# One allocator for the eight PSUM banks of a two-layer scan and attention kernel

## The chip, the core and the metric

The kernel is one program on one core of a Trainium2 chip, launched once, with all arithmetic on the chip. The metric is device time in microseconds, from the first to the last instruction; lower is better. The time before is the median of three runs, 1815.26 us (1812.67 to 1815.69).

## What is computed

Two layers, each an attention-like part and a feed-forward part, each part followed by a residual sum and a layer norm, on 2048 tokens (2 batches of 1024) of width 512, all in float32. Cut to what matters:

```
x = layernorm(x + lightning_attention(x))     # 16 heads of 32, decay per head, chunks of 128
x = layernorm(x + ffn0(x))                    # silu(x W1) * (x W3), Hadamard transform, W2; 512 -> 2048 -> 512
x = layernorm(x + selective_scan(x))          # h = exp(delta A) h + delta u B;  y = sum over 32 states of h C;  + u D
x = layernorm(x + ffn1(x))                    # silu(x Wg) * (x Wu), Wd; 512 -> 2048 -> 512

def step(h, inp):                             # the scan, per token; state is 512 channels x 32
    delta_t, B_t, C_t, u_t = inp
    dA = exp(delta_t[:, :, None] * A[None])
    h = dA * h + (delta_t * u_t)[:, :, None] * B_t[:, None, :]
    return h, einsum('bdn,bn->bd', h, C_t)
```

## The kernel before

**Tiling.** The 2048 tokens are cut into five groups of 256, 512, 512, 512 and 256 tokens (`GROUPS`). Each group runs through phases: V (values), A (attention), F (first feed-forward), the scan, and f (second feed-forward; two of the second ones are split into halves a1 and b1). Phases of different groups overlap: while VectorE (DVE), ScalarE (ACT) and GpSimd (POOL) run the scan of one group, TensorE (PE) runs the attention and feed-forward matmuls of others.

**The scan** of a group of 512 tokens has 64 units, each for one state and two blocks of 128 channels; a group of 256 tokens has 32 units, each for one state and four blocks. Per unit, POOL writes `dbu` = du * B (L1392), ACT writes `da` = exp(delta * a) block by block into PSUM (L1412: two instructions of 512 columns, or four of 256), DVE scans each block in place in PSUM (L1440), ACT keeps the last column for the next group of the same batch (L1465, which only reads `da`), and DVE multiplies `da` by C into `dbu` (L1453, which only reads `da` as well). POOL and a DMA with addition sum the results (L1483, L1489, L299).

**PSUM** has eight banks of 128 x 512 float32. The pool `ps` (L229) gives two kinds of tiles: `mm`, one bank, four buffers (L244), for every matmul output, and `da`, two banks, two buffers (L245), for the scan alone. Each use of a buffer is a tile of its own: `ps.tile(...)` is called anew for each one.

**Who reads an `mm` bank.** A matmul group is four matmuls of 512 columns (or eight of 256) into one bank. In a feed-forward phase (L1052) banks hold the gate and the up product in turn; ACT takes the silu of the one (L501), DVE multiplies by the other (L1083). The down product (L1106) is added to the residual by DVE (L1125). In attention the groups are shorter: transposes, state updates, scores, gate, outputs and norms (L729, L795, L845, L766, L891, L900, L936), read by DVE (L736, L813 and L815, L863, L919, L952) and ACT (L778, L945). Transposes (L527) are copied by ACT (L534).

**The order of work** is made when the program is built. `Order` holds one generator (thread) per phase and helper; each yields operations with an engine, an estimated duration, what is read and written, and which buffers are allocated. `run` (L166) repeatedly puts the operation that can start earliest by these estimates; `begin` (L106) says when an operation can start, among other things by when a buffer of its tag becomes free, and `put` (L129) takes the buffer, emits the instructions and moves the estimated clocks. So the emission order, and with it the order on each engine, follows estimated start times. The framework below (`manual_schedule`) keeps that order on each engine and adds the semaphore waits itself, from what the emitted instructions read and write of each tile.

`decays` (L1403) is the thread that emits the exponentials and `steps` (L1428) the one that emits the scans and products; each starts when the scan of the group before has finished with it.

Of the kernel before, what the change touches and what calls it, by code (L numbers as in the profile page):

```python
# [9 lines left out]
F32 = mybir.dt.float32  # L10
# [3 lines left out]
PSUM = bass.MemoryType.PSUM  # L14
DRAM = bass.MemoryType.DRAM

P = 128
# [3 lines left out]
G = 512  # L21
# [54 lines left out]
        self.r, self.w, self.a, self.free, self.spare = r, w, a, free, spare  # L76


class Order:


# [16 lines left out]
        self.now = 0.0  # L98

    def tag(self, name, n, make):  # L100
        self.tags[name] = (n, make, [])

    def spawn(self, gen, prio=0):
        self.new.append([gen, prio, None])

    def begin(self, op, spare=True):  # L106

        t = self.free[op.eng]
        for b in op.r:
            if b.written is None:  # L110
                return None
            t = max(t, b.written + self.HOP)
        for b in op.w:
            t = max(t, b.last + self.HOP)
        for name in {name for name, _ in op.a}:
            n, _, bufs = self.tags[name]
            k = sum(name == v for v, _ in op.a) + (op.spare if spare else 0) - (n - len(bufs))
            if k > 0:
                free = sorted(b.last for b in bufs if b.refs <= 0)
                if len(free) < k:  # L120
                    return None
                t = max(t, free[k - 1] + self.HOP)
        return t

    def switches(self, op):
# [2 lines left out]

    def put(self, op, t):  # L129
        for name, b in op.a:  # L130
            n, make, bufs = self.tags[name]
            if len(bufs) == n:
                bufs.remove(min((v for v in bufs if v.refs <= 0), key=lambda v: v.last))
            b.t = make()
            bufs.append(b)
        op.fn()
        us = op.us
        if self.switches(op):
            us += 1.3
            self.table = op.table[0]  # L140
        end = self.free[op.eng] = t + us
        if op.dma:
            q = max(self.queue[op.eng], end + 0.9) + op.dma / (
                self.QUEUE if t > self.ALONE else self.FIRST
            )
            self.queue[op.eng] = q
            end = q + 0.9
        for b in op.r:
            b.last = max(b.last, end)
        for b in op.w:  # L150
            b.last = b.written = max(b.last, end)
        for _, b in op.a:
            b.last = b.written = end
        for b in op.free:
            b.refs -= 1
        self.now = max(self.now, t)
# [56 lines left out]
def two_layers(  # L213
# [8 lines left out]
    order = Order()  # L222
# [3 lines left out]
    cp = ctx.enter_context(tc.tile_pool(name="cp", bufs=1))  # L226
    xp = ctx.enter_context(tc.tile_pool(name="xp", bufs=3 * CG))
    sm = ctx.enter_context(tc.tile_pool(name="sm", bufs=12))
    ps = ctx.enter_context(tc.tile_pool(name="ps", bufs=4, space=PSUM))  # L229
    dr = ctx.enter_context(tc.tile_pool(name="dr", bufs=1, space=DRAM))  # L230
    ring = ctx.enter_context(tc.tile_pool(name="ring", bufs=RING))

# [1 line left out]
    at = ExitStack()  # L234
# [6 lines left out]
    def tagged(name, n, pool, shape):  # L241
        order.tag(name, n, lambda: pool().tile(shape, F32, tag=name, name=name, bufs=n))

    tagged("mm", 4, lambda: ps, [P, 512])  # L244
    tagged("da", 2, lambda: ps, [P, 2, G])  # L245
    tagged("xT", 2, lambda: gp, [P, EB * G])
    tagged("xf", 1, lambda: gp, [P, EB * G // 2])
    tagged("h", 10, lambda: gp, [P, G])
# [14 lines left out]
    def chunks(gi):  # L263
        return GROUPS[gi][2]
# [8 lines left out]
    def begins(gi):  # L273
        return GROUPS[gi][1] == 0

    def ends(gi):
        return GROUPS[gi][1] + GROUPS[gi][2] == N // P
# [8 lines left out]
    def dve(cols, fn, **kw):  # L286
        return Op("DVE", 0.145 + cols * 1.05e-3, fn, **kw)

    def act(cols, fn, **kw):
        return Op("ACT", 0.18 + cols * 0.81e-3, fn, **kw)  # L290

    def pool(cols, fn, **kw):
        return Op("POOL", 0.15 + cols * 2.25e-3, fn, **kw)
# [74 lines left out]
    def take(ph, n):  # L368

        mine = of_phase[ph]  # L370
        bufs = [b for _, b, _ in mine[:n]]
        del mine[:n]
        return bufs
# [56 lines left out]
    def load_consts():  # L430
# [32 lines left out]
        def decays():  # L463
# [6 lines left out]

        raw = Buf()
        yield Op("ACT", 2.0, decays, r=[consts_b, early_b], w=[decays_b], table=EXP)
        yield dma(
            65536, lambda: a_s, lambda: alog.rearrange("(k p) n -> p k n", p=P), w=[raw]
# [28 lines left out]
    class Columns:  # L503


        def __init__(self, gi, tag="xT", cs=None):
            self.gi, self.tag = gi, tag
            self.cs = list(range(chunks(gi))) if cs is None else cs
            self.T = len(self.cs) * P
            self.whole = Buf()  # L510
            self.parts = [Buf() for _ in self.cs]
# [518 lines left out]
    def ffn(ph, xT, store, prio=0):  # L1030
# [5 lines left out]
        for fh, nt in enumerate(parts):  # L1036
# [36 lines left out]
            def hidden(f):  # L1073

                t, pg, pu = hT[f], pss[f, 0], pss[f, 1]
                yield act(
                    512, lambda: silu(t.t, pg.t), r=[pg], a=[(tag, t)], free=[pg], table=SILU
                )
                t.written = None
                if ending and f == nt - 1:  # L1080
                    reached(ph)
                yield dve(
                    512, lambda: nc.vector.tensor_mul(t.t, t.t, pu.t), r=[pu], w=[t], free=[pu]  # L1083
                )
# [128 lines left out]
    class Scan:  # L1213
# [3 lines left out]
        def __init__(self, gi):  # L1217
# [6 lines left out]
            ]  # L1224
            U = len(self.units)
            self.M = U // 2
            KP = 2 // self.R
            self.du, self.delta = [Buf() for _ in range(KP)], [Buf() for _ in range(KP)]
            self.bs, self.cs = [Buf() for _ in range(self.M)], [Buf() for _ in range(self.M)]
            self.db = [Buf() for _ in range(U)]  # L1230
            self.da = [Buf(1 if ends(gi) else 2) for _ in range(U)]
            self.ys = [Buf(), Buf()]
# [152 lines left out]
        def products(self):  # L1385
            if self.gi:
                yield lambda: scans[self.gi - 1].multiplied
            U = len(self.units)
            for i, (n, k0) in enumerate(self.units):
# [5 lines left out]
                    r=[du, bs], a=[("dbu", self.db[i])],  # L1395
                    free=([bs] if i % 2 else []) + ([du] if i + len(self.du) >= U else []),
                    prio=1,
# [5 lines left out]
        def decays(self):  # L1403
            if self.gi:
                yield lambda: scans[self.gi - 1].decayed
            U = len(self.units)
            for i, (n, k0) in enumerate(self.units):
                da, delta = self.da[i], self.delta[k0 // self.W]
                for j in range(self.W):
                    def exp():  # L1410
                        d = da.t.rearrange("p a (r t) -> p (a r) t", r=self.R)
                        nc.scalar.activation(  # L1412
                            d[:, j, :], self.wide(delta)[:, j, :], AF.Exp,
                            scale=a_s[:, k0 + j, n : n + 1],
                        )

                    yield act(
                        self.T, exp, r=[delta, scan_b] + ([da] if j else []),
                        a=[] if j else [("da", da)],
                        free=[delta] if i + len(self.delta) >= U and j == self.W - 1 else [],  # L1420
                        table=EXP,
                    )
                    self.dec[i, j].written = order.free["ACT"]
            self.decayed = True
# [3 lines left out]
        def steps(self):  # L1428
            gi, units, T = self.gi, self.units, self.T
            if gi:  # L1430
                yield lambda: scans[gi - 1].stepped
            for i, (n, k0) in enumerate(units):
                da, db, cs = self.da[i], self.db[i], self.cs[i // 2]
                d = lambda: da.t.rearrange("p a (r t) -> p (a r) t", r=self.R)
                for j in range(self.W):
                    def scan():
                        init = 0.0
                        if not begins(gi):
                            init = hlast[GROUPS[gi][0]][:, n, k0 + j : k0 + j + 1]
                        nc.vector.tensor_tensor_scan(  # L1440
                            d()[:, j, :], d()[:, j, :], self.wide(db)[:, j, :],
                            init, ALU.mult, ALU.add,
                        )

                    yield Op(
                        "DVE", 0.145 + T * 2.15e-3, scan, r=[self.dec[i, j], db, da],
                        w=[self.scanned[i]], prio=1,
                    )
                if not ends(gi):
                    spawn(self.keep_last(i))  # L1450

                yield dve(
                    1024, lambda: nc.vector.tensor_mul(  # L1453
                        self.wide(db), d(), self.row(self.cs, i)
                    ),
                    r=[da, cs], w=[db, self.out[i]], free=[da] + ([cs] if i % 2 else []), prio=1,
                )
            self.stepped = True

        stepped = False  # L1460

# [198 lines left out]
```

## Time and profile before

| | |
|---|---|
| median of the runs | 1815.26 us (1812.67 to 1815.69) |
| span of the profiled execution (the page gives no other time of it) | 1815.4 us, 0.14 us above the median |
| instructions in it | 21241 |
| granted TensorE clock, mean | 0.988 |
| busy PE, DVE, ACT, POOL | 1771.1, 1282.1, 1163.7, 1096.7 us |
| PE busy from 0 to 300 us | 290.3 us |
| PE busy from 300 to 1670 us, in which the scans lie | 1341.8 us |
| PE busy from 1670 us to the end | 139.0 us |

How to read it: the profile is of one execution. A line number is that of the kernel before. Lists of groups give engine, operation, tiles, shapes and count, then busy time and mean duration of one, then the idle time of that engine just before them and what ended it. One matmul of the kernel is two rows of the profile, so 24 matmuls appear as x48. The timeline gives the start, the duration, and in brackets the idle time before with its releaser. PEclk is the granted clock of TensorE as a share of full speed.

### The profile page before, as it was taken

The numbers are of one execution on the slowest core, as the hardware profiler recorded it, in microseconds if no ns is written. First come the engines' busy times: TensorE is split into PE (matmuls) and PEld (weight loads), VectorE is DVE, ScalarE is ACT, GpSimd is POOL, SyncE is SP. The second block draws the span as 40 slices with busy tenths as digits, with TensorE's granted clock in tenths as the row PEclk, the third lists the DMA queues.
The fourth block names the chain that finished last, engine by engine and source line by source line (L and its number), as shares of the span: only waits on it lengthen the run. The fifth ranks groups of instructions, "written<-read, shape, count | busy, mean of one in ns | idle before, by whom it ended". The sixth has DMA issues, their size and how long they took to land.

```text
span 1815.4 us, 21241 instructions
## 1 busy us (share of the span) xinstructions
PE 1771.1 (98%) x7064; PEld 1004.1 (55%) x7064; DVE 1282.1 (71%) x1537; ACT 1163.7 (64%) x1832; POOL 1096.7 (60%) x595
## 2 busy tenths in 40 slices
PE   8999999998999999999999999999999999999998
PEld 5456764443467644444666444676865444544574
DVE  3643115987599899944899999539999899998211
ACT  3734046688876676869767767686766868775311
POOL 2000015887577899935779989337998998776000
PEclk9999999999999999999999999999999999999999
DMA  9542435766648778745587787467989874766251
GB/s 283 156 139 82 151 118 168 197 164 175 210 128 253 206 207 233 200 119 185 154 221 221 199 231 212 143 213 236 275 241 262 204 213 159 199 172 168 81 174 58
DMA packets 225421, 336.32 MB, mean 185 GB/s; under 512 B 19569, under 2 KB 128897, under 8 KB 225313
## 3 DMA queue, kind: packets, MB, share of 16 engines
q1 hardware_dynamic: 206192, 270.86, 47.2%
q0 software_dynamic: 16816, 59.92, 17.6%
q10 hardware_dynamic: 2304, 4.20, 0.6%
q8 instruction: 56, 0.92, 0.2%
q14 instruction: 53, 0.43, 0.1%
HBM read 253.12 MB, written 22.54 MB: 152 GB/s over the span
## 4 chain that ended last, share of the span: by engine, by line
PE 67%; DVE 10%; ACT 8%; DMA 7%; POOL 4%; issue 3%; SPq 1%; DVEq 0%; POOLq 0%
PE mm L1052 36%; PE mm L1106 17%; DVE da L1440 6%; PE mm L658 4%; DMA y<-dbu 4%; POOL dbu L1392 3%; PE mm L1003 2%; ACT da L1412 2%; DVE dbu L1453 2%; PE mm L607 2%; ACT L501 1%; ACT L1412 1%; PE mm L845 1%; PE mm L1254 1%; PE mm L936 1%
## 5 line engine op out<-in xcount | busy, mean ns | idle before, releaser
L1392 POOL TENSOR_TENSOR dbu<-du,B 128x1024 f32<-128x1024 f32 x256 | 649.6, 2561 | 124.2 <-DMA y<-dbu 92.8
L1052 PE MATMUL mm<-xT,w 128*128 128x512 f32 (+1 forms) x1912 | 668.1, 510 | 2.9 <-ACT h L501 2.5
L1052 PEld LDWEIGHTS mm<-xT,w 128*128 128x128 f32 x1912 | 363.6, 191 | 303.9 <-issue 266.3
L1412 ACT ACTIVATE da<-delta,a_s 128x512 f32<-128x512 f32 (+1 forms) x640 | 384.4, 605 | 148.2 <-DVE dbu L1453 117.7
L1440 DVE TENSOR_TENSOR_SCAN da<-da,hlast,dbu 128x512 f32<-128x512 f32 (+1 forms) x384 | 425.8, 1109 | 36.9 <-ACT da L1412 27.7
L1489 POOL TENSOR_TENSOR y<-y,dbu 128x1024 f32<-128x1024 f32 x123 | 323.6, 2631 | 55.2 <-DVE dbu L1453 49.7
L1106 PE MATMUL mm<-w,h 128*128 128x512 f32 x768 | 339.4, 595 | 3.5 <-DMA w<-w2h 1.8
L1453 DVE TENSOR_TENSOR dbu<-da,C 128x1024 f32<-128x1024 f32 x256 | 312.9, 1222 | 13.9 <-ACT hlast L1465 7.0
L1440 DVE TENSOR_TENSOR_SCAN da<-da,dbu 128x256 f32<-128x256 f32 (+1 forms) x256 | 246.0, 961 | 26.7 <-ACT da L1412 18.8
L1106 PEld LDWEIGHTS mm<-w,h 128*128 128x128 f32 x768 | 145.2, 191 | 177.2 <-issue 164.4
L1052 PE MATMUL mm<-xf,w 128*128 128x256 f32 x1024 | 231.2, 385 | 0.2 <-DVE sc L863 0.2
L1052 PEld LDWEIGHTS mm<-xf,w 128*128 128x128 f32 x1024 | 196.7, 194 | 33.2 <-issue 4.6
L501 ACT ACT_TABLE_LOAD x143 | 183.5, 1283 | 5.1 <-PE mm L1052 2.3
L501 ACT ACTIVATE h<-mm 128x512 f32<-128x512 f32 x144 | 85.7, 597 | 114.3 <-PE mm L1052 66.3
L1083 DVE TENSOR_TENSOR h<-h,mm 128x512 f32<-128x512 f32 x96 | 65.2, 679 | 111.2 <-PE mm L1052 105.7
L1412 ACT ACT_TABLE_LOAD x109 | 139.8, 1283 | 1.9
L658 PE MATMUL mm<-xT,w 128*128 128x512 f32 (+1 forms) x320 | 116.6, 513 | 3.8 <-DVE sc L863 1.3
L299 POOL DMA_DIRECT2D y<-dbu x113 | 109.1, 966 | 12.4 <-DMA y<-dbu 5.1
L1465 ACT COPY hlast<-da 128x2 f32<-128x2 f32 (+1 forms) x160 | 25.4, 159 | 141.0 <-DVE dbu L1453 120.5
L1106 PE MATMUL mm<-w,hf 128*128 128x512 f32 x256 | 112.8, 592 | 0.0
L748 POOL TENSOR_TENSOR qd<-h,q_dec 128x512 f32<-128x512 f32 x14 | 17.8, 1271 | 151.0 <-ACT h L501 83.0
L1125 DVE TENSOR_TENSOR xn<-mm,xn 128x512 f32<-128x512 f32 x60 | 40.9, 681 | 92.9 <-PE mm L1106 92.5
(100 smaller groups left out, 1358.2 us busy)
## 6 DMA issues: line engine op xcount, KB each, us to landing
y<-dbu POOLq DMA_DIRECT2D x113, 512.0 KB, 6.0
w<-in_wgut_dram SPq DMA_DIRECT2D x192, 256.0 KB, 4.6
B<-rows SPq DMA_DIRECT2D x128, 256.0 KB, 4.6
C<-rows SPq DMA_DIRECT2D x128, 256.0 KB, 4.2
w<-in_wdnt_dram SPq DMA_DIRECT2D x96, 256.0 KB, 4.8
w<-in_w1t_dram SPq DMA_DIRECT2D x80, 256.0 KB, 4.7
w<-in_w3t_dram SPq DMA_DIRECT2D x80, 256.0 KB, 5.0
w<-w2h SPq DMA_DIRECT2D x80, 256.0 KB, 4.2
```

What stands on the lines that cost most here:

```text
L299: return Op(eng, us, lambda: of.dma_start(dst(), src(), **more), dma=nbytes, **kw)
L501: nc.scalar.activation(dst, src, AF.Silu)
L658: nc.tensor.matmul(bank.t[:, s * T : (s + 1) * T], w_qk[j][k].t[:, eb * P : (eb + 1) * P], xT.t[:, k, :], start=k == 0, stop=k == EB - 1,)
L1052: nc.tensor.matmul(bank.t[:, s * T + c0 * P : s * T + c1 * P], blocks[fb // 2][j][k // 2].t[:, k % 2 * 2 * P + k0 : k % 2 * 2 * P + k0 + P ...
L1083: 512, lambda: nc.vector.tensor_mul(t.t, t.t, pu.t), r=[pu], w=[t], free=[pu]
L1106: nc.tensor.matmul(accs[c].t, hT[f // S].t[:, s * T + c * P : s * T + (c + 1) * P], w_d[f].t, start=f == 0, stop=f == nt * S - 1,)
L1125: nc.vector.tensor_add(xb.t, bank.t, xb.t)
L1392: 1024, lambda: nc.gpsimd.tensor_mul(self.wide(self.db[i]), self.wide(du), self.row(self.bs, i)),
L1412: nc.scalar.activation(d[:, j, :], self.wide(delta)[:, j, :], AF.Exp, scale=a_s[:, k0 + j, n : n + 1],)
L1440: nc.vector.tensor_tensor_scan(d()[:, j, :], d()[:, j, :], self.wide(db)[:, j, :], init, ALU.mult, ALU.add,)
L1453: 1024, lambda: nc.vector.tensor_mul(self.wide(db), d(), self.row(self.cs, i)),
L1489: 1024, lambda: nc.gpsimd.tensor_add(y.t, y.t, db[i].t), r=o, w=[y],
```

## The change

Banks are no longer taken as tiles. The pool gives two tiles of four banks each, `mm` and `da`, allocated once, and every use takes a slice of one of them. A small allocator, `Banks`, remembers for each of the eight banks who holds it. Users of one bank may take any of the eight while no scan is open, and only the first four while one is; the scan takes bank pairs 4 and 6. A scan is open from when its `delta` is loaded (a new wait of the thread `decays`) until `steps` has emitted its last product. Where several banks are free, the one free longest is taken. The other tags keep their counts, in a class `Tiles` that does what `begin` and `put` did before.

```diff
+class Tiles:
+    def __init__(self, n, make):
+        self.n, self.make, self.bufs = n, make, []
+    def when(self, k):
+        k -= self.n - len(self.bufs)
+        if k <= 0:
+            return -1.0
+        free = sorted(b.last for b in self.bufs if b.refs <= 0)
+        return free[k - 1] if len(free) >= k else None
+    def take(self, b):
+        if len(self.bufs) == self.n:
+            self.bufs.remove(min((v for v in self.bufs if v.refs <= 0), key=lambda v: v.last))
+        b.t = self.make()
+        self.bufs.append(b)
+
+class Banks:
+    def __init__(self, views, usable):
+        self.views, self.usable = views, usable
+        self.holders = [None] * 8
+    def free_at(self, i):
+        b = self.holders[i]
+        return -1.0 if b is None else b.last if b.refs <= 0 else None
+    def of(self, width):
+        return BankTag(self, width)
+
+class BankTag:
+    def __init__(self, banks, width):
+        self.banks, self.width = banks, width
+    def places(self):
+        f, out = self.banks.free_at, []
+        for i in self.banks.usable(self.width):
+            at = [f(j) for j in range(i, i + self.width)]
+            if None not in at:
+                out.append((max(at), i))
+        return sorted(out)
+    def when(self, k):
+        free = self.places()
+        return free[k - 1][0] if len(free) >= k else None
+    def take(self, b):
+        at, i = self.places()[0]
+        b.t = self.banks.views(i, self.width)
+        for j in range(i, i + self.width):
+            self.banks.holders[j] = b
...
-        self.tags[name] = (n, make, [])
+        self.tags[name] = Tiles(n, make)
...
-            n, _, bufs = self.tags[name]
-            k = sum(name == v for v, _ in op.a) + (op.spare if spare else 0) - (n - len(bufs))
-            if k > 0:
-                free = sorted(b.last for b in bufs if b.refs <= 0)
-                if len(free) < k:
-                    return None
-                t = max(t, free[k - 1] + self.HOP)
+            k = sum(name == v for v, _ in op.a) + (op.spare if spare else 0)
+            free = self.tags[name].when(k)
+            if free is None:
+                return None
+            t = max(t, free + self.HOP)
...
-    ps = ctx.enter_context(tc.tile_pool(name="ps", bufs=4, space=PSUM))
+    ps = ctx.enter_context(tc.tile_pool(name="ps", bufs=1, space=PSUM))
...
-    tagged("mm", 4, lambda: ps, [P, 512])
-    tagged("da", 2, lambda: ps, [P, 2, G])
+    halves = [ps.tile([P, 4, G], F32, name=name) for name in ("mm", "da")]
+    opened = set()
+
+    def usable(width):
+        if width == 2:
+            return (4, 6)
+        return range(4 if opened else 8)
+
+    def views(i, width):
+        half = halves[i // 4]
+        return half[:, i % 4, :] if width == 1 else half[:, i % 4 : i % 4 + width, :]
+
+    banks = Banks(views, usable)
+    order.tags["mm"], order.tags["da"] = banks.of(1), banks.of(2)
...
+            yield lambda: self.delta[0].written is not None
+            opened.add(self.gi)
...
             self.stepped = True
+            opened.discard(self.gi)
```

## The prediction, as put on record before the changed kernel ran

> **What bounds the kernel now.** I read the page's busy times and slices first, then the chain of work, then the waits, then timelines.
>
> ```profile
> span 1815.4 us, 21241 instructions
> PE 1771.1 (98%) x7064; PEld 1004.1 (55%) x7064; DVE 1282.1 (71%) x1537; ACT 1163.7 (64%) x1832; POOL 1096.7 (60%) x595
> PE   8999999998999999999999999999999999999998
> PE 67%; DVE 10%; ACT 8%; DMA 7%; POOL 4%; issue 3%; SPq 1%; DVEq 0%; POOLq 0%
> ```
>
> TensorE (PE) is busy in all but 44 us: it is the bound, and it is nearly never late for a bank. So more banks can gain little. The PE gaps that end with a reader of a PSUM bank are the only ones that banks could shorten, and they are few: 2.5 us at L1052, 1.4 at L1106, 2.0 at L527 and a dozen under 1.3. Before the first scan PE idles 9.7 us, of which 8.4 us wait for first DMAs (4.45, 1.57, 2.39).
>
> What hides all other work is that PE runs the next group while DVE or ACT reads the bank of the last one. That holds because each use of a bank is now a tile of its own. What happens inside one tile, the scan's two-bank `da` tile shows:
>
> ```profile
> ACT hlast L1465 <- DVE dbu L1453: 120.5, 86, 3.0
> DVE dbu L1453 <- ACT hlast L1465: 7.0, 7, 1.2
> ```
>
> These are waits (total us, times, longest); next, the timeline:
>
> ```profile
> 1412.95 1.21 DVE L1453 TENSOR_TENSOR dbu<-da,C 128x1024 f32<-128x1024 f32 x1
> 1412.95 1.42 ACT L1412 ACTIVATE da<-delta,a_s 128x512 f32<-128x512 f32 x2
> 1414.47 2.62 DVE L1440 TENSOR_TENSOR_SCAN da<-da,hlast,dbu 128x512 f32<-128x512 f32 x2 [0.31 <-ACT da L1412]
> ```
>
> L1465 and L1453 only read `da`, and yet wait for each other. The first scan step at 1414.47 needs only the first exponential's bank, written by about 1413.66; DVE was free at 1414.16, and still it waited until the second exponential, in the tile's other bank, ended (1412.95 + 1.42 = 1414.37). So waits go by tile: accesses of one tile from two engines are ordered as emitted, whatever the bank, reads against reads included.
>
> **The change, part by part.** The counts of instructions stay: 3726 matmuls, 1539 on DVE, 1850 on ACT (321 table loads in both), 600 on POOL, 1009 on SP. SP and POOL issue the same DMAs in nearly the old order; at no cost, since no weight load moves ahead of a free buffer. The freedom to take eight banks while no scan is open touches only stretches that are not short of banks: worth 0 to 3 us (the sum of the few reader-ended gaps outside open scans), taken as 0.
>
> The costly part is that all uses are now slices of two tiles. I read the changed kernel's instruction order with its waits. In the four-bank tile `mm`, each of the 920 places where the emission order passes from one engine to another is ordered by a wait, and in 899 of them the two accesses are in different banks. Before, 634 of 666 were in the same bank. In the `da` tile it is 1243 places, 1038 across banks (before 500 and 275). PE resumes after another engine 436 times on `mm` and 81 on `da`: 517 handovers, 96 before the first scan, 396 while scans run, 25 after.
>
> What one handover costs: a reader of bank k is emitted after group k+1 of PE has been, because its estimated start is a hop later. So it waits for the end of group k+1, and group k+2, in another bank, waits for it. PE stands still for each reader. Behind a waiting reader on DVE stands the next scan step (L1440), for which ACT's next exponential waits, and for that the scan after it; on ACT the exponentials stand behind the silu. The durations come from these rows, of 512 columns:
>
> ```profile
> L1440 DVE TENSOR_TENSOR_SCAN da<-da,hlast,dbu 128x512 f32<-128x512 f32 x256 | 329.2, 1286 | 28.4 <-ACT da L1412 21.8 <-ACT hlast L1465 1.9 <-POOL dbu L1392 1.6
> L1453 DVE TENSOR_TENSOR dbu<-da,C 128x1024 f32<-128x1024 f32 x256 | 312.9, 1222 | 13.9 <-ACT hlast L1465 7.0
> L1412 ACT ACTIVATE da<-delta,a_s 128x512 f32<-128x512 f32 x384 | 263.3, 690 | 99.8 <-DVE dbu L1453 85.3 <-DVE da L1440 4.1 <-DMA delta<-dd 3.3
> ...
> L501 ACT ACT_TABLE_LOAD x143 | 183.5, 1283 | 5.1 <-PE mm L1052 2.3 <-ACT xn L565 0.4
> L501 ACT ACTIVATE h<-mm 128x512 f32<-128x512 f32 x144 | 85.7, 597 | 114.3 <-PE mm L1052 66.3 <-PE mm L658 28.7 <-PE mm L607 18.1
> L1083 DVE TENSOR_TENSOR h<-h,mm 128x512 f32<-128x512 f32 x96 | 65.2, 679 | 111.2 <-PE mm L1052 105.7 <-ACT h L501 4.6 <-issue 0.3
> ```
>
> A PE group is 3.46 us (the timeline has 12 in 41.60 us). A hop between DVE and ACT is 0.10 us (1414.37 to 1414.47 above); to or from PE 0.05:
>
> ```profile
> 838.66 0.60 ACT L501 ACTIVATE h<-mm 128x512 f32<-128x512 f32 x1
> 839.31 1.98 PE L658 MATMUL mm<-xT,w 128*128 128x512 f32 x4 [0.60 <-ACT h L501]
> ```
>
> With these I walked by hand through two stretches of the changed order, 17 handovers. The start of the first, a feed-forward beside a 512-token scan (us from the start of group A; the product before it ends at 1.00):
>
> ```
> PE   group A, bank 0           0.00- 3.46
> ACT  L1465 after L1453         1.10- 1.26
> DVE  L1440 after L1465         1.36- 2.64
> ACT  L1412 after L1440         2.74- 3.43
> DVE  L1083, bank 3, after A    3.51- 4.19
> PE   group B after L1083       4.24- 7.70   gap 0.78
> DVE  L1440                     4.19- 5.47
> ACT  L1412 after L1440         5.57- 6.26
> DVE  L1453 after L1412         6.36- 7.58
> ACT  L1465 after L1453         7.68- 7.84
> ACT  table load, L501, bank 0  7.84- 9.72
> PE   group C after L501        9.77-        gap 2.07
> ```
>
> Its gaps are 0.78, 2.07, 1.39, 1.55, 1.75, 2.08, 0.78, 1.18, and in a second stretch beside a scan without L1465 1.22, 0.78, 0.70, 0.78, 2.40, 0.78, 0.70, 1.12, 1.39: mean 21.45 / 17 = 1.26 us. A group thus takes 4.91 and 4.56 us instead of 3.46.
>
> The sum:
> - 396 handovers while scans run, at 1.26 us: 499 us.
> - 96 before the first scan and 25 after, at the smallest, a reader of 0.60 to 0.69 and two hops, 0.8 us: 97 us.
> - About 50 handovers hold two readers in a row (two score products L863, a silu and a copy); one more of 0.65 each: 33 us.
> - The clock. Where PE stood 2.51 us, it lost it:
>
> ```profile
> 1424.22 12.26 PE L1052 MATMUL mm<-xT,w 128*128 128x512 f32 x24 [2.51 <-ACT h L501]
> ```
> ```profile
> 1426.00:1428.00 2.00, 2.00 (x3) 0.76 (x3) 1.39 (x2) 1.95 (x4) 2.00 (x3) 0.50 0.95 230
> ```
>
>   In the second line, a window of 2 us, the granted clock is 0.50 (third number from the end), and the 12 matmuls took 12.26 instead of 10.4 us: 1.8 lost. A gap of 2.03 us at 1120 did the same, one of 1.77 at 673 did not. 3 of my 17 gaps exceed 2.0: 396 x 3/17 = 70 times 1.8 = 126 us.
>
> 499 + 97 + 33 + 126 = 755; less some 10 us of today's reader-ended gaps, 745. 1815.4 + 745 = **2560 us**. The profiled span is 0.1 us from the median, so no correction is made.
>
> A second way to it: the `da` tile's accesses in turn make a unit of 512 tokens 2 x 1.286 + 2 x 0.690 + 1.222 + 0.11 (L1465, where there is one) + 4.5 changes of engine x 0.10 = 5.7 us; in the walks, with readers between, it was 6.5 and 5.9. 192 such units at 6.2 are 1190 us, 64 of 256 tokens at an estimated 7.5 are 480: 1670 us, where the scans now lie in 1370 us together with pauses that add up to some 170. With the pauses and the stretches outside, stretched as above, that is about 2420, without clock losses. The two agree within 10%.
>
> Bounds: if each of the 517 handovers costs only 0.8 us, 1815 + 414 = 2230. If each costs the largest gap walked, 2.40, 1815 + 1241 = 3056. I take the walked mean, because it is from the order that will run.
>
> **Two rules of the Trainium skill.** The trace row of 1414.47 shows a wait across banks. "PSUM — Partial Sum Buffer", section "PSUM bank collisions raise a hardware error", says that two engines on different banks run clean, and that guarding by bank is enough. By that alone the chip needs none of the 899 waits, and the sum would be that of rival A. The instruction order has them nevertheless. "TensorE: Matmul & The Clock Gate", section "What's actually happening", lets the clock fall after an idle window of about 3.4 us; by that the clock term would be 0 and the sum 2434, while the rows lose it at 2.03 and 2.51 us.
>
> **Rivals.**
> - A, not slower. The waits are there, but their producers are done when PE comes, as four banks deep would give. PE then keeps its 98% and gains 0 to 3 us at its reader-ended gaps: 1813. For it: today's PE waits little for readers. Against it: the reader in question is the latest emitted, and itself waits for the group that has just ended. It decides from a gap under about 0.05 us; the least in my walk is 0.70. 3%.
> - B, mild. Each handover costs only reader and hops, because DVE and ACT, less loaded in a longer kernel, are always there, and the clock holds: 2230 (2150 to 2320). For it: DVE is 71% and ACT 64% busy. Against it: only 7 of 17 walked gaps were that small, as ACT's table loads stand before the silu. 11%.
> - C, two locked chains. Attention's short groups, with readers on both engines, table loads and half clock, bring the mean to the walk's largest gap: 2850 to 3056, taken as 2950. For it: the granted clock in attention is 0.50 to 0.66 already, at gaps of 0.6 to 1.2 us (1188 to 1192, 475 to 480). Against it: most handovers are of feed-forwards. 13%.
>
> The forecast, 2320 to 2850, has 73%. The range for 8 in 10 is widened a little into B: **2300 to 2850**, which leaves out C and most of B. Faster or slower means by over 0.2%, about what a measurement here can tell from no change: faster 1%, same 2% (rival A), slower 97%.
>
> **What would show it.** PE busy falls to 65 to 78% of the span while its matmul count stays; idle before L1052 and L1106, now 2.9 and 3.5 us, becomes hundreds, released by L501, L1083, L1125. DVE before L1440 waits for L1412 hundreds of us (now 46.5), ACT before L1412 for L1440. The readers' rows keep their durations. The clock shows 0.5 in parts. If PE stays above 90%, the reading of the waits is wrong; if PE's gaps are near 0.8 us, the scan's coupling is; if the clock's mean stays at 0.98, that term falls.

## The result, and the profile after

The changed kernel takes 2716.85 us (median of five runs, 2714.74 to 2720.15), the kernel before 1815.26 us on the same chip. The ratio is 1.498, with an interval of 1.496 to 1.500: 902 us slower. The forecast was 2560 us, in a range of 2300 to 2850.

The page of the changed kernel: span, busy times, the row of PE's slices, the granted clock of PE by slices, and the chain.

```profile
span 2715.1 us, 21523 instructions
PE 2044.9 (75%) x7064; PEld 1069.8 (39%) x7064; DVE 1310.3 (48%) x1537; ACT 1176.8 (43%) x1832; POOL 1101.7 (41%) x595
...
PE   8878977667667777676677787787777677677798
...
PEclk9999989887689999987699899898998899899999
...
PE 12%; DVE 10%; ACT 7%; issue 1%; DMA 0%; DVEq 0%; ACTq 0%; SPq 0%
```

The counts of matmuls and of the other engines' instructions stand where they stood, and PE, which was busy in all but 44 us, now idles in 670. DVE, ACT and POOL do the same work in the same busy time (DVE 28 us more), so nothing has become the new bound by load: no engine is above 75%. Such a page is that of engines that wait for one another. The chain could be followed back through only a third of the span, so it is not used here. PE's busy time itself grew by 274 us with the same 7064 rows, and the clock row has 6, 7 and 8 where it had 9: the second, smaller part of the loss. The mean granted clock is 0.903 (before 0.988).

The waits of the changed kernel (total us, times, longest):

```profile
ACT da L1479 <- DVE da L1507: 487.8, 241, 14.0
DVE da L1507 <- ACT da L1479: 400.4, 273, 11.4
...
ACT hlast L1533 <- DVE dbu L1520: 161.4, 94, 6.4
...
PE mm L1117 <- ACT h L566: 123.0, 65, 5.0
...
PE mm L1117 <- DVE h L1148: 72.9, 70, 2.5
...
PE mm L1171 <- DVE xn L1190: 54.5, 23, 6.4
```

Lines have moved by 65 to 68: L1117 and L1171 are the products L1052 and L1106, L566 the silu, L1148 and L1190 DVE's readers, L1479, L1507, L1520 and L1533 the exponential, the scan step, the product by C and the kept column. The exponential waits for the scan and the scan for the exponential, 241 and 273 times; that is the one `da` tile of four banks. PE waits for ACT's and DVE's readers of banks that its next group doesn't use; that is the one `mm` tile. The groups of instructions say the same from the side of the idle time (busy us, mean ns, idle us before it):

```profile
L1117 PE MATMUL mm<-xT,w 128*128 128x512 f32 x1120 | 558.2, 645 | 187.0 <-ACT h L566 107.7 <-DVE h L1148 64.0 <-DVE xn L1190 8.8
L1171 PE MATMUL mm<-w,h 128*128 128x512 f32 x672 | 341.0, 660 | 75.2 <-DVE xn L1190 46.3 <-ACT xT L599 12.0 <-ACT h L566 11.7
L1507 DVE TENSOR_TENSOR_SCAN da<-da,hlast,dbu 128x512 f32<-128x512 f32 x256 | 330.3, 1290 | 197.0 <-ACT da L1479 175.8 <-ACT hlast L1533 12.8 <-DVE dbu L1520 0.9
L1479 ACT ACTIVATE da<-delta,a_s 128x512 f32<-128x512 f32 x384 | 265.5, 691 | 391.7 <-DVE da L1507 342.0 <-DVE dbu L1520 42.5 <-ACT hlast L1533 0.6
L1148 DVE TENSOR_TENSOR h<-h,mm 128x512 f32<-128x512 f32 x90 | 61.5, 683 | 162.7 <-PE mm L1117 139.3 <-ACT h L566 8.9 <-PE mm L1336 6.8
```

The two matmul rows as they were before the change:

```profile
L1052 PE MATMUL mm<-xT,w 128*128 128x512 f32 x1160 | 502.6, 594 | 2.5 <-ACT h L501 2.5
L1106 PE MATMUL mm<-w,h 128*128 128x512 f32 x768 | 339.4, 595 | 3.5 <-DMA w<-w2h 1.8 <-DVE h L1083 1.4 <-ACT h L501 0.4
```

The means of DVE's and ACT's rows are nearly those of before (1290 after, 1286 before; 691 and 690; 683 and 679 ns): they wait and are not slowed. The matmul rows rose from 594 and 595 to 645 and 660 ns.

### The profile page after: what moved, and what is told of

Read it like the earlier page. It is cut to its first block, busy times and chain, and to the rows that moved or that the text cites. A ratio compares the mean times of both kernels' runs of the same rounds, so it can differ in the third digit from the quotient of the medians.

```text
span 2715.1 us, 21523 instructions
## 1 busy us (share of the span) xinstructions
PE 2044.9 (75%) x7064; PEld 1069.8 (39%) x7064; DVE 1310.3 (48%) x1537; ACT 1176.8 (43%) x1832; POOL 1101.7 (41%) x595
## 5 line engine op out<-in xcount | busy, mean ns | idle before, releaser
L1117 PE MATMUL mm<-xT,w 128*128 128x512 f32 (+1 forms) x1728 | 709.4, 560 | 236.6 <-ACT h L566 123.0
L1457 POOL TENSOR_TENSOR dbu<-du,B 128x1024 f32<-128x1024 f32 x256 | 628.1, 2467 | 39.3 <-DMA du<-dd 35.6
L1479 ACT ACTIVATE da<-delta,a_s 128x512 f32<-128x512 f32 (+1 forms) x640 | 387.9, 606 | 553.8 <-DVE da L1507 487.8
L1117 PEld LDWEIGHTS mm<-xT,w 128*128 128x128 f32 x1728 | 336.2, 202 | 607.9 <-issue 230.8
L1507 DVE TENSOR_TENSOR_SCAN da<-da,hlast,dbu 128x512 f32<-128x512 f32 (+1 forms) x384 | 427.2, 1113 | 271.7 <-ACT da L1479 246.7
L1557 POOL TENSOR_TENSOR y<-y,dbu 128x1024 f32<-128x1024 f32 x123 | 288.3, 2344 | 472.9 <-DVE dbu L1520 445.2
L1171 PE MATMUL mm<-w,h 128*128 128x512 f32 x672 | 341.0, 660 | 75.2 <-DVE xn L1190 46.3
L1520 DVE TENSOR_TENSOR dbu<-da,C 128x1024 f32<-128x1024 f32 x256 | 313.0, 1223 | 97.8 <-ACT da L1479 89.3
L1507 DVE TENSOR_TENSOR_SCAN da<-da,dbu 128x256 f32<-128x256 f32 (+1 forms) x256 | 246.8, 964 | 176.9 <-ACT da L1479 153.7
L1117 PE MATMUL mm<-xf,w 128*128 128x256 f32 x864 | 234.2, 432 | 55.0 <-DVE hf L1148 16.8
L1171 PEld LDWEIGHTS mm<-w,h 128*128 128x128 f32 x672 | 138.3, 212 | 265.1 <-issue 157.8
L1117 PEld LDWEIGHTS mm<-xf,w 128*128 128x128 f32 x864 | 184.6, 219 | 106.0 <-DVE hf L1148 23.3
L364 POOL DMA_DIRECT2D y<-dbu x113 | 98.6, 872 | 289.1 <-DVE dbu L1520 276.8
L1148 DVE TENSOR_TENSOR h<-h,mm 128x512 f32<-128x512 f32 x90 | 61.5, 683 | 162.7 <-PE mm L1117 139.3
L1533 ACT COPY hlast<-da 128x2 f32<-128x2 f32 (+1 forms) x160 | 25.6, 160 | 227.2 <-DVE dbu L1520 161.4
L1171 PE MATMUL mm<-w,hf 128*128 128x512 f32 x224 | 106.5, 623 | 21.2 <-DVE xn L1190 8.2
L566 ACT ACTIVATE h<-mm 128x512 f32<-128x512 f32 x123 | 73.1, 597 | 96.8 <-PE mm L1117 49.1
L723 PE MATMUL mm<-xT,w 128*128 128x512 f32 (+1 forms) x208 | 96.4, 617 | 18.1 <-DVE sc L928 11.2
L592 PE MATMUL mm<-cst,xn 128*128 128x128 f32 x208 | 39.8, 329 | 79.1 <-ACT h L566 23.4
```

What stands on the lines that cost most here:

```text
L364: return Op(eng, us, lambda: of.dma_start(dst(), src(), **more), dma=nbytes, **kw)
L566: nc.scalar.activation(dst, src, AF.Silu)
L592: nc.tensor.transpose(bank.t[:, db * P : (db + 1) * P], xn[gi, c].t[:, db * P : (db + 1) * P], ident,)
L723: nc.tensor.matmul(bank.t[:, s * T : (s + 1) * T], w_qk[j][k].t[:, eb * P : (eb + 1) * P], xT.t[:, k, :], start=k == 0, stop=k == EB - 1,)
L1117: nc.tensor.matmul(bank.t[:, s * T + c0 * P : s * T + c1 * P], blocks[fb // 2][j][k // 2].t[:, k % 2 * 2 * P + k0 : k % 2 * 2 * P + k0 + P ...
L1171: nc.tensor.matmul(accs[c].t, hT[f // S].t[:, s * T + c * P : s * T + (c + 1) * P], w_d[f].t, start=f == 0, stop=f == nt * S - 1,)
```

## The experiments

The theory behind the prediction is: **waits go by tile, and the new tiles are too large.** Its rival is: the other edits, the new emission order with opened scans and the sharing of banks, cost the time. All experiments are edits of the changed kernel. Each ran on one chip together with the kernel before; its ratio, and what is said of its distance from before, go by the time of the kernel before on that chip (1813 to 1814 us).

| | tiles over the eight banks | us | ratio to before | clock |
|---|---|---|---|---|
| before | a new one for each use | 1815.26 | 1 | 0.988 |
| changed | 4 + 4 banks | 2716.85 | 1.4982 (1.496 to 1.5004) | 0.903 |
| e4_da_split | 4 + 2 + 2 | 2400.35 | 1.3237 (1.3208 to 1.3266) | 0.946 |
| e3_mm_split | 1 + 1 + 1 + 1 + 4 | 2291.51 | 1.2637 (1.261 to 1.2663) | 0.925 |
| e8_pairs | 2 + 2 + 2 + 2 | 1950.31 | 1.0752 (1.0735 to 1.077) | 0.969 |
| e1_split | 1 + 1 + 1 + 1 + 2 + 2 | 1806.96 | 0.9962 (0.9947 to 0.9977) | 0.989 |
| e7_split_no_sharing | the same, no sharing | 1815.28 | 1.001 (0.9998 to 1.0021) | 0.991 |
| e2_no_sharing | 4 + 4, no sharing | 2931.59 | 1.6166 (1.6129 to 1.6203) | 0.880 |
| e5_three | 3 + 4, one bank set aside | 2683.66 | 1.4796 (1.4768 to 1.4825) | 0.904 |
| e6_filled | as e5, 512 columns of other matmul before groups | 2636.75 | 1.4532 (1.4497 to 1.4566) | 0.957 |
| e9_filled_half | as e6, 256 columns | 2650.29 | 1.4617 (1.4591 to 1.4642) | 0.934 |

### e1_split: the allocator kept, the tiles cut small

```diff
-    halves = [ps.tile([P, 4, G], F32, name=name) for name in ("mm", "da")]
+    ones = [ps.tile([P, G], F32, name=f"mm{i}") for i in range(4)]
+    twos = [ps.tile([P, 2, G], F32, name=f"da{i}") for i in range(2)]
...
-        half = halves[i // 4]
-        return half[:, i % 4, :] if width == 1 else half[:, i % 4 : i % 4 + width, :]
+        if i < 4:
+            return ones[i]
+        two = twos[i // 2 - 2]
+        return two[:, i % 2, :] if width == 1 else two
```

> The changed kernel with its allocator and its order untouched, but the eight banks are six tiles: four of one bank, two of two banks. Theory (waits go by tile, so slices of one four-bank tile are ordered across banks): the time falls back to 1800 to 1830 us, PE busy near 98% again, the granted clock near 0.99. Rival (the order that the new allocator gives, or banks shared by matmuls and the scan, cost the time): it stays near 2717 us, or at least above 2200.

Measured: 1806.96 us, 0.38% under before. Two lines of its page and its row of the first product:

```profile
span 1807.2 us, 21189 instructions
...
PE 1761.7 (97%) x7064; PEld 999.3 (55%) x7064; DVE 1281.1 (71%) x1537; ACT 1163.1 (64%) x1832; POOL 1096.8 (61%) x595
```
```profile
L1120 PE MATMUL mm<-xT,w 128*128 128x512 f32 x1120 | 483.7, 593 | 0.0
```

The order of emission comes from the estimated times, which know nothing of tiles, so it is that of the changed kernel (in the two traces all 7064 rows of PE stand in the same order); only the waits differ. The idle 187.0 us before the row are 0.0, and its matmuls are back from 645 to 593 ns. The whole loss lies in the size of the tiles. The rival falls. The Trainium skill, "PSUM — Partial Sum Buffer", section "PSUM bank collisions raise a hardware error", holds that guarding bank by bank suffices; this kernel, with waits by one bank or by the scan's pair, agrees with it at 1807 us.

### e2_no_sharing: the large tiles kept, the sharing taken out

```diff
-        return range(4 if opened else 8)
+        return range(4)
```

> The two four-bank tiles of the changed kernel, but single banks are always taken from the first four, as before the change; PE's order of instructions is then that of the kernel before, all 3726 matmuls. Theory: the time is that of the changed kernel, 2600 to 2850 us, since the tiles are the same. Rival (sharing of the scan's banks and the order it gives cost the time): 1815 us.

PE's order of matmuls is now the order of before (in the two traces all 7064 rows of PE stand in the same order), and yet it took 2931.59 us, above what was expected and 215 us above the changed kernel:

```profile
L1117 PE MATMUL mm<-xT,w 128*128 128x512 f32 x1160 | 582.2, 648 | 201.1 <-ACT h L566 111.3 <-DVE h L1148 65.3 <-DVE xn L1190 10.2
```

So a nearly identical row of idle time comes with the old order too, and sharing helps under large tiles: with it, users of single banks have two tiles to spread over while no scan is open, and two uses in different tiles need no wait. The first 300 us, before any scan, show it. The views of that stretch (its length, then busy us and rows of PE, PEld, DVE, ACT, POOL, then PEclk), first with no sharing, then for the changed kernel:

```profile
0.00:300.00 300.00, 208.02 (x1076) 109.18 (x1076) 78.19 (x125) 76.50 (x121) 15.01 (x25) 0.76 0.31 93
```
```profile
0.00:300.00 300.00, 248.79 (x1402) 146.94 (x1403) 92.93 (x155) 95.62 (x155) 15.01 (x25) 0.97 0.43 129
```

PE got through 1076 rows without sharing and 1402 with it (1563 before the change), and the clock is 0.76 against 0.97. The first scan step then starts at 489.9 us without sharing and at 355.3 us with it, so 135 of the 215 us are lost before any scan.

### e7_split_no_sharing: the small tiles without the sharing

The edits of e1_split and e2_no_sharing together.

> Six tiles (four of one bank, two of two), single banks always taken from the first four: the order of the kernel before, with tiles that are kept instead of allocated anew for each use. Theory (the 0.4% of the six-tile kernel come from sharing the scan's banks): 1811 to 1818 us, the same as before. Rival (they come from the kept tiles): 1805 to 1809 us.

1815.28 us, a ratio of 1.001 (0.9998 to 1.0021): no different from before. The intervals of e1_split and of this kernel don't meet; the 0.4% of e1_split thus come from sharing the banks, with the order that it gives, and not from tiles that are kept instead of made anew. That is the gain that the allocator has to give, about 7 us.

### e3_mm_split and e4_da_split: one large tile each

e3_mm_split cuts the first four banks into tiles of one and leaves the scan's four in one tile; e4_da_split does the reverse.

```diff
-    halves = [ps.tile([P, 4, G], F32, name=name) for name in ("mm", "da")]
+    ones = [ps.tile([P, G], F32, name=f"mm{i}") for i in range(4)]
+    half = ps.tile([P, 4, G], F32, name="da")
```
```diff
-    halves = [ps.tile([P, 4, G], F32, name=name) for name in ("mm", "da")]
+    half = ps.tile([P, 4, G], F32, name="mm")
+    twos = [ps.tile([P, 2, G], F32, name=f"da{i}") for i in range(2)]
```

> The changed kernel with four one-bank tiles for the matmuls, but the scan's four banks still one tile. Theory: PE's handovers are free again, ACT and DVE still take turns in the scan at 5.7 to 6.5 us per unit of 512 tokens; the scans, now 1370 us with their pauses, take 1670 to 1840, so 2050 to 2300 us, PE busy about 80 to 86%, DVE waiting for ACT at the scan step some 300 us as in the changed kernel. Rival (the handovers of PE alone make the loss): below 1900 us.

> The changed kernel with one four-bank tile for the matmuls, but the scan's banks as two tiles of two. Theory: each of 436 handovers still stops PE for a reader and two hops, 0.8 to 1.1 us, as ACT and DVE are no longer locked to each other: 350 to 480 us and a clock loss of 50 to 130, so 2200 to 2430 us. Rival (the scan's turns alone make the loss): below 1900 us.

2291.51 us (478 over before) and 2400.35 us (587 over), both within what was expected. The waits of e3_mm_split, and then the groups of e4_da_split:

```profile
ACT da L1481 <- DVE da L1509: 384.7, 245, 5.2
DVE da L1509 <- ACT da L1481: 377.1, 325, 3.0
```
```profile
L1120 PE MATMUL mm<-xT,w 128*128 128x512 f32 x1120 | 529.3, 617 | 123.0 <-DVE h L1151 53.1 <-ACT h L569 51.6 <-ACT hlast L1536 13.4
L1510 DVE TENSOR_TENSOR_SCAN da<-da,hlast,dbu 128x512 f32<-128x512 f32 x256 | 329.3, 1286 | 47.4 <-ACT da L1482 42.7 <-ACT hlast L1536 1.6
```

Each large tile is costly by itself. With the scan's tile large, exponential and scan lock each other as in the changed kernel, although the matmul banks are free of it. With the `mm` tile large, the scan's idle time before L1510 is 47.4 us (before 28.4, changed 197.0), and PE stands still for readers: 414 gaps of 1.10 us in the mean, 286 of them under 0.9 us. In the changed kernel the mean gap is 1.51. So the locked scan lengthens the gaps of PE, because the reader for which PE waits stands behind a scan's instruction that waits itself: of the 434 gaps that DVE or ACT ended in the changed kernel, 151 were ended by an instruction that starts over 0.3 us after PE stopped and comes right behind one of the scan on its engine (table loads aside), and their mean is 2.24 us; in e4_da_split it is 48 of 410. Alone the two cost 478 + 587 = 1065 us, together 902: part of their stalls lies side by side.

### e8_pairs: four tiles of two banks

```diff
-    halves = [ps.tile([P, 4, G], F32, name=name) for name in ("mm", "da")]
+    twos = [ps.tile([P, 2, G], F32, name=f"{n}{i}") for n in ("mm", "da") for i in range(2)]
...
-        half = halves[i // 4]
-        return half[:, i % 4, :] if width == 1 else half[:, i % 4 : i % 4 + width, :]
+        two = twos[i // 2]
+        return two[:, i % 2, :] if width == 1 else two
```

> The changed kernel with four tiles of two banks each. In the matmul tiles some 600 of 890 places where the engine changes are still ordered across banks. Theory (PE stands only when its next group shares a tile with the bank being read and with the group that just ended): with two tiles taken in turn there is nearly always a group that may go on, so 1805 to 1840 us. Rival (each wait across banks costs, whatever the tile): two thirds of the handovers' loss of 587 us in the kernel whose matmul tile alone is whole, so about 2200 us.

1950.31 us: neither number was met. Most of the loss goes with two tiles instead of one, since groups that follow each other mostly lie in different tiles, but 137 us stay. PE has 101 gaps of 130 us in all (changed 439 and 664). Its waits, from the longest sum on:

```profile
PE mm L592 <- ACT xn L630: 15.0, 9, 3.0
PE mm L1117 <- ACT mm L1011: 11.6, 4, 4.1
PE mm L1117 <- ACT h L566: 11.2, 7, 4.8
PE mm L1171 <- DVE xn L1190: 6.8, 7, 2.7
PE mm L1001 <- ACT sg L991: 6.7, 4, 3.2
```

They are spread out. The feed-forward products L1117 and L1171 still have 43 of the 130 us, 11.2 of them behind the silu (123.0 in the changed kernel) and 0.2 at L1117 behind DVE's product (72.9); the rest lies at transposes (L592), in attention (L1001), and where ACT writes a bank (L1011). That short groups come back to a pair sooner is argued from the code, not shown by a run.

### e5_three, e6_filled and e9_filled_half: what the gaps cost in clock

e5_three sets one bank aside, so that it can hold the output of matmuls that nobody needs. e6_filled issues one of these, of 512 columns, before each operation that takes an `mm` bank while a scan is open: 380 more matmuls, whose output is unused. It doesn't wait, since nothing else touches its bank. e9_filled_half makes it 256 columns.

```diff
+    spare_bank = ps.tile([P, G], F32, name="spare")
-    halves = [ps.tile([P, 4, G], F32, name=name) for name in ("mm", "da")]
+    halves = [ps.tile([P, n, G], F32, name=name) for n, name in ((3, "mm"), (4, "da"))]
+    nc.vector.memset(spare_bank, 0.0)
...
-        return range(4 if opened else 8)
+        return (0, 1, 2) if opened else (0, 1, 2, 4, 5, 6, 7)
```
```diff
-        return Op("PE", us, fn, **kw)
+        def filled():
+            if opened and any(name == "mm" for name, _ in kw.get("a", ())):
+                nc.tensor.matmul(
+                    spare_bank, wbc_s[:, 0, :], wbc_s.rearrange("p k o -> p (k o)"),
+                    start=True, stop=True,
+                )
+            fn()
+
+        return Op("PE", us, filled, **kw)
```

> The changed kernel with one bank of the matmul tile set aside in a tile of its own, unused, so three are left in the tile: the control of the next one. Theory: handovers stay as many (412 on the matmul tile), since the order across banks and not their number sets the gaps: 2650 to 2850 us, clock 0.89 to 0.91. Rival (banks are short): above 2900.

> The control with 380 more matmuls, one of 512 columns (0.87 us at full clock) into the bank set aside ahead of each matmul group that takes a bank while a scan is open; they wait for nothing and add work that the output does not use. Theory (about 240 us of the loss is TensorE at half clock after gaps): PE stays active through most gaps, mean clock 0.95 or more, the wanted matmuls' mean durations fall back towards those of the kernel before (595 and 594 ns for L1106 and L1052 of 512 columns), and the time falls by 50 to 200 us below the control, although 331 us of matmuls are added. Rival (the rows are longer for another reason, such as refilling the array after each stop): no gain in the clock-bound rows, and the time rises by 50 to 330 us.

> The three-bank kernel with 380 added matmuls of 256 columns (0.43 us at full clock) instead of 512. Theory (the clock is lost in gaps over 2 us, and the long fill overran the common gaps of 0.78 us): no fill overruns, but a gap of 2.5 us still leaves 2.1 idle, so the clock's mean lies between 0.904 and 0.957, at 0.92 to 0.94, and the time between 2600 and 2670 us. Rival (the fills' own time is all that counts): slower than the three-bank kernel's 2684 us by up to 160 us.

e5_three: 2683.66 us, a little faster than with four banks, so the changed kernel isn't short of banks. e6_filled: 2636.75 us, 47 less than e5_three, just under what was expected, and that with more work on PE. e9_filled_half: 2650.29 us, 33 less, its clock 0.934 between the others'. The first product without filling, and then, with filling, the first product and the filling itself:

```profile
L1119 PE MATMUL mm<-xT,w 128*128 128x512 f32 x1088 | 539.2, 642 | 179.7 <-ACT h L568 98.8 <-DVE h L1150 63.8 <-DVE xn L1192 11.5
```
```profile
L1127 PE MATMUL mm<-xT,w 128*128 128x512 f32 x1088 | 520.5, 623 | 82.0 <-ACT h L576 61.3 <-DVE h L1158 16.2 <-DVE xn L1200 1.9
L353 PE MATMUL spare<-wbc 128*128 128x512 f32 x760 | 409.5, 621 | 0.0
```

PE is busy 2255.6 us with filling; without the 409.5 us of L353 that is 1846.1, against 2032.9 in e5_three: the wanted matmuls take 187 us less, of the 262 us by which e5_three's exceed those of before. This gives the time in which rows of the two overlap to the filling; the rows of the wanted matmuls alone cover 1926.9 us, 106 less. PE's idle time falls by 267 us (643 to 376), the filling takes 409.5, and 409.5 - 187 - 267 = -44 is the change of the span. What PE lost at half clock (half of its busy time in the stretches that the trace records at a clock of 0.50) falls from 204 to 103 us, 17 of them in the filling. So the filling, which leaves the waits between engines as they are, shows that a large part of PE's longer busy time, 106 to 187 of the 262 us, is a cost of standing still; and that it is a cost beside the gaps themselves.

## Why the prediction was right, and where it was off

The mechanism and the side were right; one term of the sum was sized at about half.

**Waits go by tile: right.** e1_split is the direct proof, since it changes the tiles alone: 2717 to 1807 us.

**517 handovers: about right.** The trace shows 439 gaps of PE, 268 of them before the feed-forward products L1117 and L1171. Idle time is thus also in the short groups of attention, which the two walks didn't contain: 664 us of gaps, 396 of them at these two lines.

**The walk: right in form.** This is the stretch of the first walk on the chip (start, duration, and in brackets the gap before and its releaser):

```profile
1668.33 3.70 PE L1117 MATMUL mm<-xT,w 128*128 128x512 f32 x8 [1.12 <-ACT h L566]
1672.81 3.70 PE L1117 MATMUL mm<-xT,w 128*128 128x512 f32 x8 [0.78 <-DVE h L1148]
1678.09 3.70 PE L1117 MATMUL mm<-xT,w 128*128 128x512 f32 x8 [1.58 <-ACT h L566]
1682.82 3.70 PE L1117 MATMUL mm<-xT,w 128*128 128x512 f32 x8 [1.03 <-DVE h L1148]
1687.88 3.70 PE L1117 MATMUL mm<-xT,w 128*128 128x512 f32 x8 [1.36 <-ACT h L566]
1692.84 3.70 PE L1117 MATMUL mm<-xT,w 128*128 128x512 f32 x8 [1.25 <-DVE h L1148]
1698.52 5.40 PE L1117 MATMUL mm<-xT,w 128*128 128x512 f32 x8 [1.98 <-ACT h L566]
1704.69 3.70 PE L1117 MATMUL mm<-xT,w 128*128 128x512 f32 x8 [0.78 <-DVE h L1148]
1709.25 0.66 PE L592 MATMUL mm<-cst,xn 128*128 128x128 f32 x4 [0.86 <-ACT h L566]
```

The eight gaps after the first group sum to 9.62 us, where the walk had 11.58; silu and product alternate as releasers, and the shortest is 0.78, as walked. But groups take 3.70 us and not 3.46, which was the time of groups that follow each other without a gap, and one takes 5.40. From the first group's start to the end of the eighth gap it is 40.92 us, walked 39.26. The hop between DVE and ACT, which the walk took from one row as 0.10 us, is 0.03 to 0.04 us in the median of these waits in both traces; those to and from PE are 0.04 to 0.06, as walked. Over the whole kernel the gaps are longer, 1.51 us, against 629 / 517 = 1.22 of the forecast's idle terms; 105 exceed 2 us, where the walk's share gave 70.

**The idle terms: right in sum.** 499 + 97 + 33 - 10 = 619 us more of idle PE were forecast; it is 670 - 44 = 626. This agreement is closer than the parts deserve: fewer gaps than counted and longer ones than walked offset each other.

**The clock: the step that failed.** It was forecast as 70 x 1.8 = 126 us, and PE's busy time rose by 274. The trace records the clock as either full or half, so the cost can be added up: half of PE's busy time in the stretches at half clock is 213 us, before the change 19. The clock thus took 194 of the 274; the other 80 are left for groups that restart at full clock, 3.70 for 3.46 us, a price that the forecast put at nothing (an estimate from 0.24 us at each of some 400 more gaps is 97). Of 70 x 1.8 the second factor holds: groups after a gap of over 2.5 us take 5.38 us in the mean instead of 3.70, 1.7 lost. The first is low, with 105 gaps over 2 us. The trace also tells where the 194 lie: 123 at the feed-forward products L1117 and L1171 (131, before 8), nearly what was forecast for all, and 71 at all other lines (82, before 12), most of them attention's, where the forecast named a clock of 0.50 in the old trace and gave it no price. With the measured 274 in place of 126, the sum is 745 - 126 + 274 = 893 of the 900 us between the spans.

The rule weighed in the prediction, that the clock falls after an idle window of about 3.4 us (the Trainium skill, "TensorE: Matmul & The Clock Gate", section "What's actually happening"), fits these runs in the window's length and not in its being idle throughout: above, a gap of 1.98 us is followed by a group of 5.40 us, and the last section counts such windows. The same page's section "A second HAM failure mode: psum-queue depth-cycling" says that frequent short idles between matmul groups make the clock go up and down, and e6_filled agrees: less idling, clock 0.904 to 0.957.

**The second way, 2420 us: too low.** Its units of 6.2 and 7.5 us were right as medians: in the changed kernel the median step from one unit's product L1520 to the next is 6.24 us for 512 tokens and 7.31 for 256. But the means are 8.5 and 8.2, as 13 steps take over 15 us, 474 us in all, some 390 more than 13 units would take; 170 of pauses were put in and stretched. It also had no clock.

**Sharing at nothing: right for the old tiles, not for the new.** With small tiles it gives 0.4 to 0.5% (e1_split against before and against e7_split_no_sharing), 0 to 3 us having been forecast and 7 to 9 found; in the large tiles it saves 215 us (e2_no_sharing). The forecast had that inside its count of handovers already, since it counted them in the order with sharing; the traces have 439 gaps of PE with sharing and 563 without.

**The rivals.** A (not slower) fell with the 664 us of gaps. B (2230, each gap just reader and hops) was nearly that of e4_da_split, where the scan isn't locked: 286 of 414 gaps under 0.9 us, and 2400 us. In the changed kernel 199 of 439 are. C (2950) asked for a mean gap of 2.40 us; it is 1.51.

**What would show it.** PE's 75% is in the 65 to 78 named; DVE waits for ACT at the scan for 400.4 us and ACT for DVE 487.8; the readers' durations stand. The idle time "in the hundreds" is 187.0 us at L1117 and only 75.2 at L1171.

## What to carry to other kernels

Make a tile as small as what must be ordered: banks that different engines use at the same time belong in different tiles, even where one allocator hands them all out. Before such a change, count in the built order the places where the emission passes from one engine to another within a tile, and how many of them are across buffers; walking through a dozen with the durations of the old trace gives the idle time. Then price the clock apart, for gaps of about 2 us and more, and in the stages of short groups as well, and the restart of each group after a gap.

## What the runs showed of the hardware

- In all eleven traces the granted clock is 0.50 or 1.00 and changes only on a grid of 3.41 us. Here are four such windows from the stretch of the walk in the changed kernel (length, then busy us and rows of PE, PEld, DVE, ACT, POOL, then PEclk):

```profile
1692.46:1695.87 3.41, 3.03 (x7) 1.44 (x8) 2.84 (x3) 0.63 (x3) 1.42 (x1) 1.00 1.05 265
1695.87:1699.29 3.42, 1.44 (x4) 0.49 (x3) 1.29 (x1) 3.38 (x4) 3.27 (x2) 1.00 0.16 57
1699.29:1702.70 3.41, 3.41 (x5) 1.35 (x4) 1.23 (x1) 1.32 (x3) 0.68 (x2) 0.50 0.00 0
1702.70:1706.11 3.41, 2.63 (x7) 0.89 (x6) 1.89 (x2) 0.24 (x1) 2.57 (x2) 1.00 0.68 174
```

  In the second window PE is busy for 1.44 us, 42% of it, as the gap of 1.98 us lies wholly inside. The third has half the clock, though PE is busy in all of it; half of 3.41 is the 1.7 us that the group of 5.40 lost. Over the eleven traces half clock followed all of 382 full-clock windows in which PE was busy for less than 40%, 102 of 215 from 40 to 50%, and 38 of 5952 above. Full clock came back after 1 of 329 half-clock windows that were busy for less than 80%, 41 of 80 from 80 to 90%, and 477 of 509 above.
- The length of one gap therefore decides only in part. In the changed kernel the four-matmul groups of 512 columns at L1117, L1171 and L723 that came after a gap ran slow (over 4.2 us instead of 3.70) in 6 of 78 cases after gaps under 0.9 us, 3 of 38 up to 1.5, 0 of 8 from 1.5 to 1.8, 2 of 7 up to 2.0, 7 of 19 from 2.0 to 2.5, and 23 of 29 above 2.5 us, where the mean group took 5.38 us. Going by the counts above, what matters is how much of one window is idle, by this gap and its neighbours together.
- PE can gain by work that nobody needs: 380 matmuls in the gaps took 409.5 us and made the kernel 47 us faster. It is still 1.45 times the kernel before; mending the waits is worth 910 us.
- The version that beats both kernels is e1_split, 1806.96 us: the allocator over tiles of one bank, and of two for the scan.
